# Two graph layers on one core: the opening by half blocks, loads of A at release, chunk ends in three cycles, and a rearranged seam between set-up and first pass

## Chip, core and metric

The kernel runs on one core of a Trainium2 chip. The time is the device time of one execution in microseconds; for a kernel several executions are made and the median is given. The profile is one further execution, recorded by the hardware profiler. Engines are named as in the profile: PE (TensorE, matrix products), DVE (VectorE), ACT (ScalarE), POOL (GpSimd), SP (SyncE). PEld is PE's weight load. SP, ACT and POOL also issue DMA transfers; each issues its own in order.

## The reference, cut to what matters

N is 4096 nodes, F 512 features, H 8 heads of 64. The first layer is graph attention over a dense 0/1 matrix A (`adj`), the second attends within 32 graphs of 128 nodes; both have a residual and a layer norm.

```python
# layer 0
feats   = einsum('nf,hfo->hno', X, W)
s_self  = einsum('hno,ho->hn', feats, a_self)
s_neigh = einsum('hno,ho->hn', feats, a_neigh)
dense = s_self[:, :, None] + s_neigh[:, None, :]
dense = where(dense > 0, dense, 0.2 * dense) * A[None]
attn = softmax(dense, axis=-1)
out = relu(concat_heads(einsum('hij,hjo->hio', attn, feats) + b))
x = layernorm(x + out)
# layer 1
a = where(same_graph, (x Wq^T + bq) (x Wk^T + bk)^T / sqrt(512), 0)
scores = (a + A + A) * where(same_graph, 1, -1e6)
x = layernorm(x + (softmax(scores) * same_graph) @ (x Wv^T + bv))
```

## The kernel before

**Set-up.** The rows of x are taken in 8 blocks of four tiles of 128 rows. `load_rows(k)` loads the four tiles of block k into the pool `xtp`, which has four buffers, so that a block's loads wait for the turning of the one before. `turn_rows(k)` (line 641) transposes them on PE (L650), four tiles by four column groups, and ACT copies the result to `xT` (L653) and sums it on the way. `features(k, u)` (line 715) multiplies a tile by W (L722) into one of two buffers of PSUM; DVE adds b (L733). W has two more columns per head, W a_self and W a_neigh, which DVE computes (L634, L635) from W and from broadcast copies of a_self and a_neigh; with them the product yields the scores too. In block 0 the first three tiles don't wait for these columns: `first_scores` (line 741) gives their scores afterwards, by 24 products of 16 columns (L746). `exponentials` makes e_all, pu_j and d_all; `scaled_features` (line 757) makes g (L766) and f in two parts (L775, L776), which POOL stores in DRAM as g_d and f_d (L789), once for two tiles. `parts_of_exponentials` splits values into bf16 parts on DVE (L676 to L690), `rows_of_exponentials` transposes pu_j and stores pu_d (L695, L699, L703), `columns_of_exponentials` turns the rows back (L708). `partial_sums` and `sums_to_columns` (L561, L568) sum the features over all nodes.

**Passes.** Four passes follow (r, `main_pass`, line 1326), each for two heads. A pass goes over 4 chunks (c) of 1024 targets and, in each, over 32 steps (j) of 128 sources; in the first three passes in cycles of 8 steps, so a chunk has four cycles. In a cycle:

- SP loads f_s and g_s (L1367, L1371), one of each for four steps, into two buffers each. At a chunk's beginning it loads p_row and u_row (L1331, L1334), broadcast rows of pu_d.
- DVE makes q (128 x 1024, L1386) for every step and head. It needs A^T of the step (`at`), p_row and d_all.
- ACT makes mark from q (L1395); for one q of eight DVE does it (L1391).
- PE multiplies f_s with `at` (accf, L1406), g_s with q (acc, L1426) and e_b with mark (dens, L1441); in pass 0 also e_p with `at` (ae, L1350).

**A^T.** In pass 0 `bring` (line 1116) makes `at`. `load_adjacency` (line 577) loads four steps of A for a chunk as fp8 on POOL (L581) into one of three buffers a_b; PE turns two steps at once as bf16 pairs (L1130); ACT casts each to fp32 (L1134); POOL stores it to at_d (L1135), from where SP reads it in later passes. Half of the next cycle's steps are brought behind accf, half at the cycle's end. The tiles `at` and q come from rings of 6 buffers (`ring`, line 550), to which the first three passes add 6 and 2 (`more_at`, `more_q`), in memory that set-up has left.

**Chunk ends.** After a chunk, `sums_to_rows` (line 1171) evacuates accf and acc on DVE (L1180, L1188) and dens and ae on ACT (L1190, L1195). The rest comes in pieces between the next chunk's cycles: transposes and sums of ae (L1203, L1214), those of dens, then the output rows (L1260, L1261) and their store to hs_d (L1271). `run_pieces` gives each cycle a credit, and each piece yields a cost; it runs pieces while the credit is above zero.

**Order.** PE's instructions are issued as the program has them (`manual_schedule`). For the other engines and queues a planner chooses the order when the kernel is built, apart from instructions marked `keep_in_program_order`. The seam in the program is: last features, parts, rows of the last block (L695), L568, columns (L708), then pass 0, which begins by bringing steps 0 to 7. The tile `hst` (pool `hp_`, one buffer) holds both the evacuated ae and the output rows.

Of the kernel before, what the change touches and what calls it, by code (L numbers as in the profile page):

```python
# [19 lines left out]
P = 128  # L20
# [384 lines left out]
def adjacency_streamed_path(  # L405
# [144 lines left out]
    def ring(name, pool, n):  # L550

        if name not in more:
            return pool
        k = turns[name] % (n + more[name][1])
        turns[name] += 1
        return pool if k < n else more[name][0]
# [14 lines left out]

    ats = {}
    a_bs = {}
    pools = {}
# [10 lines left out]

    with tc.tile_pool(name="setup1", bufs=1, side="right") as one, tc.tile_pool(
        name="setup2", bufs=2, side="right"
    ) as two, tc.tile_pool(name="xtp", bufs=4, side="right") as xtp, tc.tile_pool(
        name="setup_rows", bufs=1, side="right"
    ) as late, tc.tile_pool(name="staged", bufs=3, side="right") as staged, tc.tile_pool(  # L590
# [9 lines left out]
        def load_rows(k):  # L600
            xts[k] = []
            for u in range(4):
                xt = xtp.tile([P, F], F32, name="xt_f")
                queue = nc.scalar if k else nc.sync
                queue.dma_start(xt, x[ts(4 * k + u, P), :])
                xts[k].append(xt)

        load_rows(0)
        FW = FH + 2
        w_sb = one.tile([P, FC, H, FW], F32, name="w_sb_f")  # L610
        for c in range(FC):
            nc.scalar.dma_start(
                w_sb[:, c, :, :FH], W[:, ts(c, P), :].rearrange("h p o -> p h o")
            )
        a_b2 = staged.tile([P, PR, 2, 2, FP], F32R, name="fst").bitcast(F32)
        a_b2 = a_b2[:, :2].rearrange("p r u s n -> p (r u s n)").rearrange(
            "p (k h o) -> p k h o", k=2, h=H
        )
        for k, v in enumerate((a_self, a_neigh)):
            nc.sync.dma_start(  # L620
                a_b2[:, k].rearrange("p h o -> p (h o)"), broadcast_rows(v, P, H * FH)
            )
        b_row = one.tile([P, H * FH], F32, name="b_row")
        nc.sync.dma_start(b_row, broadcast_rows(b, P, H * FH))
        b_col = one.tile([P, PR], F32, name="b_col")
# [4 lines left out]
        load_rows(1)  # L630
        for c in range(FC):
            prod = qp.tile([P, C], F32, name="q").rearrange("p (k h o) -> p k h o", k=2, h=H)
            for k in range(2):
                nc.vector.tensor_mul(prod[:, k], w_sb[:, c, :, :FH], a_b2[:, k])  # L634
                nc.vector.tensor_reduce(w_sb[:, c, :, FH + k], prod[:, k], AX.X, OP.add)  # L635
# [3 lines left out]
        xs = one.tile([P, FC, NB], F32, name="xs")  # L639

        def turn_rows(k):
            xT = xTs[k] = two.tile([P, FC, 4, P], F32, name="xT_f")
            pts = {}

            order = [(u, c) for u in range(4) for c in range(FC)]
            for u, c in order if k == 0 else sorted(order, key=lambda x: x[1]):
                if u == 0:
                    last = k == 0 and c == FC - 1
                    pts[c] = misc([P, 4, P]) if last else pss.tile([P, 4, P], F32, name="ps_set")
                nc.tensor.transpose(pts[c][:, u, :], xts[k][u][:, ts(c, P)], ident)  # L650
            for c in range(FC):
                pt = pts[c]
                nc.scalar.activation(  # L653
                    xT[:, c], pt, AF.Identity, accum_out=xs[:, c, k : k + 1]
                )

        def exponentials(k, u, sc):
# [5 lines left out]
            for lo, hi, w in ((0, 3, 1), (3, 5, 0)):  # L663
                nc.vector.tensor_tensor(
# [27 lines left out]
        def rows_of_exponentials(k):  # L692
# [5 lines left out]
            row = rows[k] = late.tile([2 * H, 4 * P], F32, name="pu_row")  # L698
            nc.scalar.copy(  # L699
# [5 lines left out]
        def columns_of_exponentials(k):  # L705
            pc = pss.tile([P, 4, 2 * H], F32, name="ps_set")
# [8 lines left out]
        def features(k, u):  # L715
            pf = psf.tile([P, 2, HB], F32, name="ps_fe")
            pf = pf[:, :, : H * FW // 2].rearrange("p q (h w) -> p q h w", w=FW)
            scored = k > 0 or u == 3
            cols = slice(0, FW if scored else FH)
            for c in range(FC):  # L720
                for q in range(2):
# [6 lines left out]
                    )  # L728
            if u % 2 == 0:
# [11 lines left out]
        def first_scores():  # L741

            ps = pss.tile([P, 4, H, 2], F32, name="ps_set")
            for u in range(3):
# [9 lines left out]
            for u in range(3):  # L754
                exponentials(0, u, ps[:, u].rearrange("p (q h) w -> p q h w", q=2))

        def scaled_features(k, u):
            j, v, i = 4 * k + u, u // 2, u % 2
            fb = sums[k, v][:, i]
            if i == 0:  # L760
                pairs[k, v] = (
                    qp.tile([P, C], F32, name="q").rearrange("p (r u n) -> p r u n", r=PR, u=2),
                    staged.tile([P, PR, 2, 2, FP], F32R, name="fst"),
# [12 lines left out]
            nc.vector.scalar_tensor_tensor(  # L776
# [774 lines left out]
```

## Time and profile before

| | |
|---|---|
| median of 3 runs | 2066.62 us (2066.22 to 2067.95) |
| profiled execution, its time | 2068.04 us |
| its span | 2066.2 us |
| granted PE clock, mean over the span | 0.995 |
| set-up, to the end of the last features | 0 to 156.8 us |
| first accf group starts | 165.2 us |
| first accf group of pass 1 starts | about 592 us |
| ACT busy in 180 to 220 us | 37.45 of 40 us |
| DVE busy in 180 to 220 us | 35.15 of 40 us |
| loads of a_b (L581), issue to landing, median | 16.3 us |
| stores of at_d (L1135), issue to landing, median | 14.9 us |
| DMA read and written | 491.8 and 107.2 MB |

The span runs from the first to the last instruction that the profiler saw. A group row of the profile shows how often a line's instruction ran, its busy time and the mean of one, and the idle time of its engine just ahead of it with what ended that. A row of waits has the total, the number and the longest. A row of windows gives PE, PEld, DVE, ACT and POOL busy time, then the granted PE clock (1.00 is full), the DMA share and GB/s.

### The profile page before, as it was taken

What the parts mean: (1) busy time and instruction counts of PE and PEld (TensorE: products, weight loads), DVE (VectorE), ACT (ScalarE), POOL (GpSimd) and SP (SyncE); (2) the same over time, 40 slices, a digit from 0 to 9 for tenths busy, and PEclk for the clock granted to TensorE, in tenths of its full rate; (3) what the DMA queues carried; (4) which work ended last, traced back from release to release, by engine and by line L of the source; (5) the groups of instructions that cost most, each with busy time, mean ns of one, the idle gap of its engine ahead of it and who ended that gap; (6) DMA issues with size and microseconds to landing.
All of it is one profiled execution on the core that took longest, in us unless ns stands there. A gap on an engine that the chain in (4) does not pass through costs nothing.

```text
span 2066.2 us, 38253 instructions
## 1 busy us (share of the span) xinstructions
PE 2030.9 (98%) x15086; PEld 1049.8 (51%) x15086; DVE 1670.1 (81%) x2125; ACT 1540.4 (75%) x1869; POOL 222.9 (11%) x361
## 2 busy tenths in 40 slices
PE   8999999999999999999999999999999999999997
PEld 6885555444445444444445444444454445445443
DVE  5667888888799998798999899998975884896654
ACT  3338888888878899788899899998885666567420
POOL 1223222222100000000000000000210210210111
PEclk9999999999999999999999999999999999999999
DMA  6989999999899999798999899989974773684211
GB/s 195 303 270 248 270 294 263 296 260 297 264 341 335 367 347 350 258 312 293 327 308 338 300 354 329 329 287 360 315 247 150 240 262 128 229 275 167 74 49 43
DMA packets 207371, 551.31 MB, mean 267 GB/s; under 512 B 24780, under 2 KB 65740, under 8 KB 207180
## 3 DMA queue, kind: packets, MB, share of 16 engines
q1 hardware_dynamic: 136716, 418.45, 58.1%
q0 software_dynamic: 62272, 121.91, 23.1%
q10 hardware_dynamic: 8192, 8.39, 1.2%
q8 instruction: 121, 1.98, 0.4%
q14 instruction: 70, 0.57, 0.1%
HBM read 491.79 MB, written 107.22 MB: 290 GB/s over the span
## 4 chain that ended last, share of the span: by engine, by line
PE 84%; DMA 7%; issue 4%; DVE 2%; ACT 1%; POOL 1%; POOLq 0%; ACTq 0%; DVEq 0%; SPq 0%
PE acc L1426 36%; PE accf L1406 20%; PE ps_m L1067 5%; PE ps_fe L722 5%; PE ps_m L995 5%; DMA at_d<-at 5%; PE dens L1441 5%; PE ps_m L1022 1%; DVE q L1386 1%; PE ps_m L1081 1%; DMA xt_f<-in_x_dram 1%; ACT mark L1395 1%; PE ps_m L975 1%; PE ps_m L1130 1%; PE ps_m L924 1%
## 5 line engine op out<-in xcount | busy, mean ns | idle before, releaser
L1386 DVE SCALAR_TENSOR_TENSOR q<-p_row,d_all,at 128x1024 f32<-128x1024 f32 x1024 | 1241.9, 1277 | 159.9 <-PE acc L1426 129.3
L1395 ACT ACTIVATE mark<-q,nb_all 128x1024 fp8e4<-128x1024 f32 x896 | 995.5, 1145 | 181.4 <-DVE q L1386 165.8
L1426 PE MATMUL acc<-q,g_s 128*32 128x512 f32 x8192 | 904.2, 593 | 1.4 <-DVE q L1386 0.4
L1426 PEld LDWEIGHTS acc<-q,g_s 128*32 128x32 f32 x8192 | 264.3, 110 | 595.3 <-issue 533.6
L1406 PE MATMUL accf<-at,f_s 128*128 128x512 f32 x2048 | 496.7, 398 | 1.9 <-issue 1.8
L1406 PEld LDWEIGHTS accf<-at,f_s 128*128 128x128 f32 x2048 | 380.5, 189 | 111.4 <-issue 28.1
L1151 ACT ACTIVATE ck<-ck,neg_half_f 128x1024 f32<-128x1024 f32 x128 | 146.0, 1141 | 21.7 <-DMA ck<-in_adj_dram 21.7
L1152 ACT ACTIVATE ck<-ck,neg_quarter 128x1024 f32<-128x1024 f32 x128 | 146.4, 1143 | 1.7
L1441 PE MATMUL dens<-mark,e_b 128*6 128x512 fp8e4 x2048 | 125.9, 379 | 0.9 <-ACT mark L1395 0.9
L722 PE MATMUL ps_fe<-w_sb_f,xT_f 128*128 128x264 f32 (+1 forms) x512 | 121.3, 394 | 4.6 <-ACT xT_f L653 4.6
L1134 ACT CAST at<-ps_m 128x1024 fp32r<-128x1024 fp8e4 x128 | 120.1, 1026 | 5.5 <-ACT mark L1395 3.0
L1067 PE MATMUL ps_m<-wvT,x1T 128*128 128x512 f32 x256 | 114.2, 594 | 0.0
L995 PE MATMUL ps_m<-x1T,M_sb 128*128 128x512 f32 x256 | 112.9, 595 | 0.0
L722 PEld LDWEIGHTS ps_fe<-w_sb_f,xT_f 128*128 128x128 f32 x512 | 100.7, 200 | 19.1 <-ACT xT_f L653 5.0
L1271 POOL DMA_DIRECT2D hs_d<-hst x12 | 10.7, 893 | 834.4 <-DVE hst L1261 816.1
L1391 DVE TENSOR_SCALAR mark<-q,d_all 128x1024 fp8e4<-128x1024 f32 x128 | 95.7, 748 | 4.8
L1441 PEld LDWEIGHTS <-e_b 128*6 128x6 bf16 x2048 | 55.8, 86 | 78.5 <-issue 36.2
L1135 POOL DMA_DIRECT2D at_d<-at x128 | 69.0, 539 | 178.0 <-ACT at L1134 107.4
L995 PEld LDWEIGHTS ps_m<-x1T,M_sb 128*128 128x128 f32 x256 | 48.0, 190 | 59.3 <-issue 58.4
L1067 PEld LDWEIGHTS ps_m<-wvT,x1T 128*128 128x128 f32 x256 | 47.6, 190 | 56.4 <-issue 55.1
L1075 DVE TENSOR_TENSOR v_t<-ps_m,bv_row 128x512 f32<-128x512 f32 x32 | 21.7, 683 | 60.5 <-PE ps_m L1067 60.5
L1002 ACT ACTIVATE zT<-ps_m,zb 128x512 f32<-128x512 f32 x32 | 21.8, 680 | 61.1 <-PE ps_m L995 61.1
(185 smaller groups left out, 1084.2 us busy)
## 6 DMA issues: line engine op xcount, KB each, us to landing
at<-at_d SPq DMA_DIRECT2D x384, 512.0 KB, 6.0
f_s<-f_d SPq DMA_DIRECT2D x128, 512.0 KB, 7.5
at_d<-at POOLq DMA_DIRECT2D x128, 512.0 KB, 14.9
ck<-in_adj_dram SPq DMA_DIRECT2D x128, 512.0 KB, 5.4
g_s<-g_d SPq DMA_DIRECT2D x128, 256.0 KB, 5.7
f_d<-fst POOLq DMA_DIRECT2D x16, 1024.0 KB, 7.2
a_b<-in_adj_dram POOLq DMA_DIRECT2D x32, 512.0 KB, 16.3
p_row<-pu_d SPq DMA_DIRECT2D x32, 512.0 KB, 6.7
```

What stands on the lines that cost most here:

```text
L722: nc.tensor.matmul(pf[:, q, :, cols], tile_j(xTs[k][:, c].rearrange("p u n -> p (u n)"), u), w_sb[:, c, 4 * q : 4 * q + 4, cols], start=(c ...
L995: nc.tensor.matmul(pz, L1["M"][:, f, ts(c, P)], x1T[:, f, :], start=(f == 0), stop=(f == FC - 1),)
L1067: nc.tensor.matmul(pv, x1T[:, f, ts(u, P)], L1["wvT"][:, f, :], start=(f == 0), stop=(f == FC - 1),)
L1134: nc.scalar.copy(at, both[:, :, k])
L1151: tc.keep_in_program_order(nc.scalar.activation(ck, ck, AF.Square, bias=neg_half))
L1152: nc.scalar.activation(ck, ck, AF.Abs, bias=neg_quarter, accum_out=binp[:, k : k + 1])
L1386: nc.vector.scalar_tensor_tensor(q, p_row[h], d_j, ats[r, c, j].bitcast(F32), op0=OP.max, op1=OP.mult)
L1391: nc.vector.tensor_scalar(mark, q, d_j, None, op0=OP.is_gt, saturate=False)
L1395: nc.scalar.activation(mark, q, AF.Sigmoid, bias=nb_all[:, j, hh : hh + 1], scale=BIG, saturate=False,)
L1406: nc.tensor.matmul(accf[:, s, :], f_s[j // 4][:, j % 4, w, :], ats[r, c, j][:, ts(s, HB)], start=(j == 0 and w == 0), stop=(j == NT - 1 an ...
L1426: nc.tensor.matmul(acc[o : o + 32, s, :], g_s[j // 4][:, j % 4, h, o % FH : o % FH + 32], qs[j, h][:, ts(s, HB)], start=(j == 0), stop=(j ...
L1441: nc.tensor.matmul(dens[lo : lo + 6, :], e_b[:, j, 2 * r + h, :], marks[j, h][:, ts(s, HB)], start=(j == 0), stop=(j == NT - 1),)
```

## The change

The opening:

- Block 0 is loaded, turned and copied in two halves of two tiles. The second half is turned in the middle of the features of tile 1. Two of W's four loads go to SP; every load of x is on SP; a_self and a_neigh lie in two separate staging buffers. An activation of `neg_quarter` stands ahead of ACT's copies. PE transposes the identity nine times ahead of tile 0 and twice ahead of tile 1.
- All four tiles of block 0 get their scores from `first_scores`, now 32 products, and it runs behind tile 3 (it ran behind tile 2). The score columns of the last two groups of W are pinned on DVE behind the additions of tiles 0 and 1.

The seam:

- Steps 0, 2 and 4 (each with its neighbour) are turned during the last block, behind tiles 1, 2 and 3, and steps 0 to 4 are cast there. Step 6 is turned behind L568, ahead of the last rows. Step 5's cast and the last scaled features are placed behind the copy of these rows; steps 6 and 7 are cast at the beginning of pass 0.
- The first cycle's q and marks are told from which instruction on they may be issued. The last block's `parts_of_exponentials` come behind the q of the first cycle, its columns (L708) behind the first accf.
- Staging is split into pools of one and two buffers, the added `at` buffers into pools of two and four; the order of the set-up pools differs. The first loads of f_s, g_s, p_row and u_row are kept in program order.

The first pass:

- When a block of A has been turned, the load that takes its buffer is issued then, in program order; the loads for steps 12 and 16 of chunk 0 stand at the end of set-up.
- `run_pieces` gets 8 instead of 6 a cycle in pass 0; each piece still yields 6 (the last 1.8).

```diff
+    def turned_steps(c, j, pt):
+        if j % 4 == 0 and (c, j) not in a_bs:
+            load_adjacency(c, j)
...
+        for t in range(CT):
+            nc.tensor.transpose(pt[:, t, :], pairs[:, t, :], ident_b)
+        ahead = c * NT + j + 10
+        if j % 4 == 2 and ahead < NCH * NT and (c or j > 6):
+            tc.keep_in_program_order(load_adjacency(ahead // NT, ahead % NT))
+        return pt
+    def cast_steps(c, j, pt, steps=range(2)):
...
+        for k in steps:
+            at = ats[0, c, j + k] = ring("at", atp, 6).tile([P, C], F32R, name="at")
+            ends_of_setup["ACT"] = nc.scalar.copy(at, both[:, :, k])
+            nc.gpsimd.dma_start(at_d[c, j + k], at.bitcast(F32))
...
-                queue = nc.scalar if k else nc.sync
-                queue.dma_start(xt, x[ts(4 * k + u, P), :])
+                nc.sync.dma_start(xt, x[ts(4 * k + u, P), :])
...
-        load_rows(0)
+        load_rows(0, (0, 1))
...
-            nc.scalar.dma_start(
+            queue = nc.scalar if c < FC // 2 else nc.sync
+            queue.dma_start(
                 w_sb[:, c, :, :FH], W[:, ts(c, P), :].rearrange("h p o -> p h o")
             )
...
+        nc.scalar.activation(neg_quarter, neg_quarter, AF.Identity)
...
+            nc.sync.dma_start(a_s[k], broadcast_rows(v, P, H * FH))
+        load_rows(0, (2, 3))
...
+            def keep_warm(n):
+                pw = psf.tile([P, 2, HB], F32, name="ps_fe")
+                for i in range(n):
+                    nc.tensor.transpose(pw[:, 0, :P], ident, ident)
...
+                if (k, c) == (0, 0) and u < 2:
+                    keep_warm((9, 2)[u])
...
+                if (k, u, c) == (0, 1, 1):
+                    turn_rows(0, (2, 3))
...
-            for u in range(3):
+            for u in range(4):
                 for c in range(FC):
                     nc.tensor.matmul(
                         ps[:, u],
...
+                if k == 0 and u < 2:
+                    score_columns(FC // 2 + u)
-                if u == (0 if k else 2) and k + 1 < NB:
+                if u == (0 if k else 3) and k + 1 < NB:
                     turn_rows(k + 1)
...
+                if k == NB - 1 and u:
+                    bank = ps0 if u == 1 else pss
+                    pt = bank.tile([P, CT, P], BF16, name="ps_m" if u == 1 else "ps_set")
+                    pt = turned_steps(0, 2 * u - 2, pt)
+                    cast_steps(0, 2 * u - 2, pt, range(2 if u < 3 else 1))
...
-        columns_of_exponentials(NB - 1)
+        last_pair = turned_steps(0, 6, misc([P, CT, P], BF16))
+        rows_of_exponentials(NB - 1)
+        with tc.issue_after(ends_of_setup["ROW"].ins):
+            cast_steps(0, 4, pt, range(1, 2))
+            scaled_features(NB - 1, 3)
+        for j in (12, 16):
+            tc.keep_in_program_order(load_adjacency(0, j))
...
-                    run_pieces(0.75 * wide)
+                    run_pieces((0.75 if r else 1.0) * wide)
...
                 if at_step == 0:
-                    for j in cycle:
-                        bring(0, 0, j)
+                    cast_steps(0, 6, last_pair)
...
+                        with following(at_step == 0, ("DVE", 3 if j else 2)):
+                            ends_of_setup["Q"] = nc.vector.scalar_tensor_tensor(
+                                q, p_row[h], d_j, ats[r, c, j].bitcast(F32), op0=OP.max, op1=OP.mult
+                            )
...
+                            with following(at_step == 0, "ACT", "ROW"):
...
+                if at_step == 0:
+                    with following(True, "Q"):
+                        parts_of_exponentials(NT // 4 - 1)
...
+                if at_step == 0:
+                    columns_of_last()
...
+    more["at"], more["q"] = [(atp, 6)], [(qp, 6)]
+    for name, n in (("at", 2), ("at", MORE - 2), ("q", 2)):
+        pool = wide_passes.enter_context(tc.tile_pool(name=f"more_{name}{n}", bufs=n))
+        more[name].append((pool, n))
```

`following` opens `tc.issue_after` for the named instruction, so that what is inside is issued behind it; `in_order` pins an instruction to the program's order.

## The prediction

> **What bounds the kernel now.** I read the page's busy shares first, then TensorE's (PE) own waits, then two-microsecond windows for the granted clock, and last PE's instructions in order of time around the seam between set-up and the first pass.
>
> ```profile
> PE 2030.9 (98%) x15086; PEld 1049.8 (51%) x15086; DVE 1670.1 (81%) x2125; ACT 1540.4 (75%) x1869; POOL 222.9 (11%) x361
> ...
> PE ps_set L650 <- DMA xt_f<-in_x_dram: 6.4, 4, 3.9
> PE ps_fe L722 <- ACT xT_f L653: 4.6, 1, 4.6
> PE ps_m L1130 <- ACT at L1134: 2.0, 2, 1.2
> ...
> PE accf L1406 <- issue: 1.8, 1, 1.8
> PE ps_set L695 <- ACT pu_j L671: 1.3, 1, 1.3
> ```
>
> PE is idle for 2066.2 - 2030.9 = 35.3 us only, and its busy work hardly changes. So the change can win only idle time (each row: total, times, longest, in us) and half-clock time, or create new ones.
>
> ```profile
> 30.00:32.00 2.00, 2.00 (x10) 1.79 (x10) 0.60 (x6) 0.86 (x9) 0.00 (x0) 0.61 0.98 325
> 32.00:34.00 2.00, 2.00 (x6) 1.52 (x6) 0.00 (x0) 0.69 (x3) 0.00 (x0) 0.53 0.41 156
> ...
> 164.00:166.00 2.00, 1.61 (x10) 1.51 (x10) 2.00 (x4) 2.00 (x3) 1.23 (x3) 0.50 1.01 373
> 168.00:170.00 2.00, 2.00 (x6) 1.52 (x5) 2.00 (x2) 2.00 (x3) 0.18 (x1) 0.50 1.02 395
> ```
>
> The third number from the right is the granted clock. In finer windows it is 0.5 from 30.5 to 33.8 (3.4 us) and from 160.1 to 170.4 (10.3 us, three times 3.4): whole stretches of one length. The first follows 24 thin matmuls (L746, 16 columns), during which PE counts as busy; the second follows the patchy seam:
>
> ```profile
> 152.96 3.83 PE L722 MATMUL ps_fe<-w_sb_f,xT_f 128*128 128x264 f32 x16
> 156.63 0.49 PE L695 MATMUL ps_set<-ident_f,pu_j 128*16 128x128 f32 x3
> 158.45 0.28 PE L695 MATMUL ps_set<-ident_f,pu_j 128*16 128x128 f32 x1 [1.33 <-ACT pu_j L671]
> ...
> 159.80 1.59 PE L1130 MATMUL ps_m<-ident_b,a_b 128*128 128x128 bf16 x16
> 162.56 1.01 PE L1130 MATMUL ps_m<-ident_b,a_b 128*128 128x128 bf16 x8 [1.16 <-ACT at L1134]
> 164.39 1.01 PE L1130 MATMUL ps_m<-ident_b,a_b 128*128 128x128 bf16 x8 [0.82 <-ACT at L1134]
> 165.16 9.99 PE L1406 MATMUL accf<-at,f_s 128*128 128x512 f32 x32
> ```
>
> The last features end at 156.8; the first accf group starts 8.4 us later and takes 9.8 us in the chain, against 7.36 us for the next one.
>
> **Start: 4.0 us, from 0 to 8.** In the old order all 16 transposes of x (L650) come first, spread from 3.9 to 9.3 us over four arriving tiles; then PE waits 4.6 us, because ACT, sitting in its queue on loads of the next x tiles, begins its table load at 11.89 and its copies at 13.19. The new order needs two x tiles, has those later loads on SP, and loads the table early. The two x tiles were down by 5.7 us; eight transposes at the cold 0.22 us and a half-width copy (0.6 us for the full width, so about 0.4) put the first features at about 6.7. W is the doubt: its loads took 6.3 to 9.9 us, so I take 7.2. From there: four feature groups at 48 x 0.2156 = 10.35 us per three, so 13.8; the other eight transposes 0.94; the turning of block 1 1.87; scores 32 x 0.1275 (3.06 / 24) = 4.08; the next feature group 3.57. That is 24.3 us warm. To it I add the cold opening, 12.03 - 10.35 = 1.68; about 0.2 of waiting; and 2.2 for a clock drop after the scores (below). End: 7.2 + 28.4 = 35.6, against 39.6 now: 4.0. VectorE (DVE) has 10.9 us of score columns (8 x 1.36) and can start at about 9 us, when a_self is down; with the additions of L733 (0.69 each) between, it ends near 21, before the scores at about 22 to 24. If W or DVE is 4 us late, nothing is won here.
>
> Two rules of the page "TensorE: Matmul & The Clock Gate" speak against this part. **The eleven added warming transposes:** the old trace has PE transposing for 63% of 6.6 to 10.0 us, and the features still run at half speed until about 17 us (matmul records of 797 ns at first, 378 ns later). This leaves open whether full density would have raised the clock. Part 4 of the page, on PE-mode transposes, says that transposes do not engage the full clock. By a reading of the row that blames only the gaps I would save the 1.68 us; by the rule nothing. I take nothing. **The longer scores:** now there are 1.87 us of transposes and 3.06 us of thin matmuls, and one half-clock stretch follows, worth 3.4 x 0.5 = 1.7 us. The new stretch is 5.95 us. Part 1's section on what is happening gives a free-running window of about 3.4 us, which agrees with the stretches above, and which a longer thin stretch fills more surely. One window costs 1.7 us, two cost 3.4; I take 2.2.
>
> **Set-up blocks: 1.2 us, from 0 to 1.3.** Of the 6.4 us that PE waited for x, 1.24 us lie at 92.7: loads issued on ACT at 76.5 to 77.9 landed only at 92.6. They shared the DMA queues with row broadcasts that SP had sent at 73.5 to 76.5 (p_row, u_row). The change pins those, and the first f_s and g_s, behind the x loads on SP, and SP issues x as soon as a buffer is free. What is queued behind a waiting x load is then only needed at the seam, 60 us later.
>
> **Seam: 6.2 us, from 3 to 8.** From the end of the last features (156.79) to the second cycle's accf (193.94) is 37.15 us. Its PE work, warm, is: L695 0.44, L568 0.79, L708 0.35, four turned pairs of steps 1.83, accf 7.36, two pairs 0.91, acc 13.9, dens 1.73, ae 0.92, two pairs 1.0; sum 29.2. Two pairs move into the last set-up block; they cost the same there (0.92 in all). So at most 37.15 - 29.2 = 7.9 us can go: 3.3 us of waits shown above, the rest slow clock. The new order fills the 1.33 us wait for pu_j with a pair of steps, L568 and another pair (0.46 + 0.79 + 0.46). L708 and the parts go behind accf and the Qs. PE then has only about 2.2 us of light work before accf, hardly more than the 1.93 us of a set-up turning that never cost the clock, so no half-clock stretch is expected.
>
> What is late next? *ACT:* five casts (1.02 each) now lie in set-up, where it is busy 6.4 of 20 us. It still owes three casts, a table load (1.28) and 14 marks (1.145 each), 20.4 us with no gap, from about 161.3; so the marks end near 182 to 184, and dens (acc start 168.5 + 13.9) wants them at 182.4. *DVE:* in the old run eight q stood ready 4.5 us before acc; now acc starts 7.5 us sooner, while the first q can start only some 5 us sooner. The sixth q takes the buffer whose g_d store is issued after the last scaled features; stores landed in 4.0 to 7.4 us, so that q comes at about 168 to 169, just before acc, and up to 2 us are lost. I book 1.7 us for both: 7.9 - 1.7 = 6.2. The loads of A for steps 12 and 16 go out on POOL behind these stores; a store of at_d behind them waits 0.9 us each, and its buffer is not needed for a cycle.
>
> **First pass: 2.4 us, from 0.5 to 3.** The old chunk ends spread over four cycles (6 credits a cycle). The last piece falls into the chunk's last cycle: its two DVE products (L1261, 2.56 us) run just ahead of the evacuation of accf (L1180), for which accf at 592.3 waits 1.76 us. Its store of hs_d still holds the buffer that ACT wants for L1195 (12.1 us of waits in all), and dens then waits for marks 0.66 and 0.22 us. With 8 credits the pieces run in cycles one to three, a cycle (26 us) earlier, so both lose their cause: 2.64 us, less something for new small waits. The loads at release win nothing on PE: POOL waited 100.3 us for PE at L581 in the first 560 us, yet PE never waited for a_b. A pinned load follows transposes that its own casts need too, so it delays at_d by its issue alone.
>
> **Sum.** 4.0 + 1.2 + 6.2 + 2.4 = 13.8 us of the profiled span of 2066.2 us, around which 1.8 us lie (its time is 2068.0). That execution was 1.4 us above the median of the runs, 2066.6; I subtract from the median: 2066.6 - 13.8 = **2052.8 us**.
>
> **Rivals.**
> 1. *The cover is thinner* (0.22): DVE or W late at the start (gain 1), q and marks late at the seam (gain 3.5), chunk ends 1.5, blocks 1: 7 us, **2059.6**. For it: ACT is busy 17 to 20 of every 20 us after 160. Against it: eight q buffers, and DVE idle for 6.5 us at 178.
> 2. *The clock stays full* (0.17): dense transposes do raise it (1.7) and the scores do not drop it (2.2), seam near 7.5: 13.8 + 5.2 = 19 us, **2047.6**. For it: set-up turnings of 1.93 us never dropped it. Against: the rule, and the 0.5 at 30.5.
> 3. *Slower: the early A loads choke the seam* (0.05): two blocks of 2 MB in the reference's type, issued back to back at about 161, overtake the last g_d store, and the sixth q waits for a landing like a_b's (16.3 us in the page) in place of 5. The q queue stands, acc comes 11 us late, and PE drops to half clock again (10.3 us, as now, 5 us lost). 16 us against the 13.8: **2069**. It decides the sign once that store lands later than 19 us. Against it: the store goes first on the same queue.
> 4. *The scheduler puts casts or Qs no earlier than before* (0.06): start, blocks and chunk ends alone, about 7.6, less 3 of mixing: **2062**.
>
> The main case has 0.50, its own range 2050 to 2056. For eight in ten I go from 2047.0 to 2060.0, which holds it, most of rivals 1 and 2. Two tenths of a per cent, 4.1 us, is what a measurement here tells from no change. Faster: 0.50 + 0.17 + nearly all of 0.22 and half of rival 4: 0.91; within: 0.05; slower: 0.04.
>
> **What would show it.** Right: the first L722 near 7 us; no wait at L650 near 90; accf's first 32 records in about 7.4 us at clock 1.00, starting some 2.2 us behind the last features; no 1.76 us at the end of the first pass. Wrong: L722 waiting on W or DVE; a half clock behind the last features; q of L1386 waiting on the g_d store; dens waiting on ACT marks in the first cycle by over 2 us.

## The result, and the profile after

| | before | after |
|---|---|---|
| median of 6 runs, us | 2067.21 (2064.97 to 2070.18) | 2055.14 (2053.82 to 2057.91) |
| profiled execution: time, span, us | 2068.04, 2066.2 | 2057.91, 2056.1 |

The changed kernel takes 0.9943 [0.993, 0.9956] of the time, 12.1 us less. The execution that was profiled is the longest of its six, so the two traces differ by 10.1 us only. Both numbers are needed below.

PE's line in the page's busy shares, with the other engines, for the changed kernel:

```profile
PE 2030.4 (99%) x15105; PEld 1051.0 (51%) x15105; DVE 1671.9 (81%) x2125; ACT 1542.2 (75%) x1878; POOL 224.2 (11%) x361
```

PE's work has not changed (2030.9 us before), its idle time went from 35.3 to 25.7 us. PE's own waits of the changed kernel (total, times, longest, in us):

```profile
PE accf L1499 <- ACT at L621: 2.1, 1, 2.1
PE ps_m L1075 <- DVE x1b L520: 1.9, 1, 1.9
PE ps_fe L800 <- ACT xT_f L723: 1.9, 2, 1.6
PE ps_m L610 <- DVE pu_all L787: 1.7, 1, 1.7
PE ps_fe L714 <- POOL ident_f masks.py:199: 1.4, 1, 1.4
PE ps_set L720 <- DMA xt_f<-in_x_dram: 1.0, 3, 0.5
...
```

The waits for x (6.4 us), for the copies of xT (4.6 us) and for the pass boundary ("issue", 1.8 us) have shrunk or gone. Three rows are new. One is the wait of the added warming transposes for the identity (L714), at the very start. The other two lie in the seam: the first accf group (L1499) waits 2.1 us for a cast on ACT, and a turned pair of A (L610) waits 1.7 us for DVE. The granted clock, the third number from the right, in two-microsecond windows of the changed kernel:

```profile
30.00:32.00 2.00, 2.00 (x8) 1.79 (x8) 1.06 (x7) 0.84 (x8) 0.00 (x0) 0.50 0.24 92
32.00:34.00 2.00, 2.00 (x6) 1.49 (x6) 2.00 (x6) 0.62 (x5) 0.18 (x1) 0.50 0.01 4
...
158.00:160.00 2.00, 2.00 (x7) 1.52 (x7) 2.00 (x3) 1.98 (x3) 1.99 (x3) 0.61 0.60 236
160.00:162.00 2.00, 2.00 (x7) 1.58 (x6) 2.00 (x3) 1.99 (x3) 2.00 (x4) 0.54 0.91 317
```

Both half-clock stretches are still there. In one-microsecond windows the one behind the scores lasts from 28.7 to 35.6 (twice 3.4 us, where it was one) and the one of the seam from 158.4 to 161.9 (one, where it was three).

**Where the time went.** I put four marks on PE in both traces and take differences: the turning of block 2 (its first L720), that of block 6, the second cycle's accf, and the first accf of pass 1. Here they are in the kernel before and in the changed one:

```profile
39.47 2.09 PE L650 MATMUL ps_set<-ident_f,xt_f 128*128 128x128 f32 x16
109.53 2.04 PE L650 MATMUL ps_set<-ident_f,xt_f 128*128 128x128 f32 x16
193.75 7.55 PE L1406 MATMUL accf<-at,f_s 128*128 128x512 f32 x32
592.31 7.59 PE L1406 MATMUL accf<-at,f_s 128*128 128x512 f32 x32 [1.76 <-issue]
...
36.76 2.09 PE L720 MATMUL ps_set<-ident_f,xt_f 128*128 128x128 f32 x16
105.36 2.03 PE L720 MATMUL ps_set<-ident_f,xt_f 128*128 128x128 f32 x16
187.43 7.60 PE L1499 MATMUL accf<-at,f_s 128*128 128x512 f32 x32
581.76 7.60 PE L1499 MATMUL accf<-at,f_s 128*128 128x512 f32 x32
```

| stretch of PE | before, us | after, us | gain | forecast |
|---|---|---|---|---|
| start to turning of block 2 | 39.47 | 36.76 | 2.7 | 4.0 |
| to turning of block 6 | 70.06 | 68.60 | 1.46 | 1.2 |
| to second accf (the seam) | 84.22 | 82.07 | 2.15 | 6.2 |
| to first accf of pass 1 | 398.56 | 394.33 | 4.23 | 2.4 |
| rest | 1473.9 | 1474.3 | -0.4 | 0 |

The three middle stretches are firm: in another profile of the changed kernel (e9), and in the experiments that leave them alone, they came out at 68.59 to 68.61, 82.07 to 82.08 and 394.24 to 394.38. The one exception is the seam of e8, with 83.73: there accf ran at full clock, the second of the new waits grew to 3.26 us, and the half clock came behind it. The first stretch is not firm. Over eight profiles with this same opening the mark lies between 33.67 and 37.13, with a mean of 35.1, so against the one profile of the kernel before the gain at the start is 4.3 us on average and 2.7 in the profile shown. The rest, which the change doesn't touch, is not firm either: it lies between 1471.5 and 1474.5 us, with a mean of 1473.0 over the same eight profiles (in the profile shown one more half-clock stretch falls between 1984 and 1988). With the means for both the sum is 4.3 + 1.46 + 2.15 + 4.23 + 0.9 = 13.0. The medians differ by 12.1 here, and by 14.2 when the changed kernel was run again (e9), so the table accounts for the gain to about a microsecond, and not to a tenth.

So the total came out near the forecast by two errors against each other: the seam gave a third of what was booked, and the first pass almost twice. The timeline of the changed kernel at the seam, all engines (start, duration, engine, line, operands; in brackets the idle time before it and what ended it):

```profile
154.64 0.61 PE L610 MATMUL ps_m<-ident_b,a_b 128*128 128x128 bf16 x8
...
155.08 0.60 PE L768 MATMUL ps_set<-ident_f,pu_j 128*16 128x128 f32 x4
...
155.32 1.01 ACT L621 CAST at<-ps_m 128x1024 fp32r<-128x1024 fp8e4 x1
...
156.23 0.59 ACT L777 COPY hst<-ps_set 16x512 f32<-16x512 f32 x1
156.73 0.99 ACT L621 CAST at<-ps_set 128x1024 fp32r<-128x1024 fp8e4 x1
...
157.77 9.18 PE L1499 MATMUL accf<-at,f_s 128*128 128x512 f32 x32 [2.09 <-ACT at L621]
157.90 0.48 DVE L934 MEMSET dens<- 128x512 f32 x1 [1.75 <-ACT at L621]
...
158.89 9.65 DVE L1475 SCALAR_TENSOR_TENSOR q<-p_row,d_all,at 128x1024 f32<-128x1024 f32 x8
...
166.88 0.42 PE L786 MATMUL ps_m<-ident_f,hst 16*128 16x16 f32 x4
...
169.25 0.22 DVE L787 COPY pu_all<-ps_m 128x64 f32<-128x64 f32 x1
169.52 0.61 PE L610 MATMUL ps_m<-ident_b,a_b 128*128 128x128 bf16 x8 [1.67 <-DVE pu_all L787]
```

Read it backwards. The accf group goes over the steps 0 to 7 in order, and the casts of steps 0 to 4 were done by 155, so it had data to begin with. What it has to wait for is ACT reading PSUM, the memory that PE writes its products to: step 5's cast at 156.73 reads a bank of the set-up pool (ps_set), and ACT comes to it only behind the cast of step 6 and the copy of the last rows (the change itself put it behind that copy). The filling of dens with zeros (L934), which reads no data at all, waits for the same cast. (Whether one bank is waited for or the whole set-up pool, the trace doesn't tell.) At the other end of accf, the last columns (L786) go into the shared bank ps_m; DVE copies them out (L787) behind all eight q and a mark of its own, at 169.25, and the next pair of A needs that bank. Neither wait is for data. Between the two lies the half-clock stretch, because of which accf took 9.18 us.

### The profile page after: what moved, and what is told of

It reads as the page before. It is cut to its first block, busy times and chain, and to the rows that moved or that the text cites. A ratio compares the mean times of both kernels' runs of the same rounds, so it can differ in the third digit from the quotient of the medians.

```text
span 2056.1 us, 38302 instructions
## 1 busy us (share of the span) xinstructions
PE 2030.4 (99%) x15105; PEld 1051.0 (51%) x15105; DVE 1671.9 (81%) x2125; ACT 1542.2 (75%) x1878; POOL 224.2 (11%) x361
## 4 chain that ended last, share of the span: by engine, by line
PE 93%; DVE 4%; issue 1%; DMA 1%; SPq 0%; POOL 0%; ACT 0%; POOLq 0%; DVEq 0%
PE acc L1521 41%; PE accf L1499 23%; PE ps_fe L800 5%; PE ps_m L1167 5%; PE dens L1536 5%; PE ps_m L1095 5%; DVE q L1475 3%; PE ps_m L1122 1%; PE ps_m L610 1%; PE ps_m L1181 1%; PE ps_m L1075 1%; PE ps_m L1024 1%; PE ps_m L1339 1%; PE ps_set L720 1%; PE ae L1435 1%
## 5 line engine op out<-in xcount | busy, mean ns | idle before, releaser
L1499 PE MATMUL accf<-at,f_s 128*128 128x512 f32 x2048 | 495.2, 398 | 2.1 <-ACT at L621 2.1
L1499 PEld LDWEIGHTS accf<-at,f_s 128*128 128x128 f32 x2048 | 380.3, 188 | 110.4 <-issue 26.4
L800 PEld LDWEIGHTS ps_fe<-w_sb_f,xT_f 128*128 128x128 f32 x512 | 100.1, 199 | 16.4 <-ACT xT_f L723 2.5
## 6 DMA issues: line engine op xcount, KB each, us to landing
at_d<-at POOLq DMA_DIRECT2D x128, 512.0 KB, 14.8
```

The costliest lines, as they stand in the source:

```text
L800: nc.tensor.matmul(pf[:, q, :, cols], tile_j(xTs[k][:, c].rearrange("p u n -> p (u n)"), u), w_sb[:, c, 4 * q : 4 * q + 4, cols], start=(c ...
L1499: nc.tensor.matmul(accf[:, s, :], f_s[j // 4][:, j % 4, w, :], ats[r, c, j][:, ts(s, HB)], start=(j == 0 and w == 0), stop=(j == NT - 1 an ...
```

## The experiments

A ratio is against the kernel before, run beside it on the same chip: e1 to e4 on one chip, e5 to e8 on a second, e9 to e12 on a third. The changed kernel itself lay 12.1 us under the kernel before in the first runs and 14.2 us in e9's, so a difference of two microseconds between these groups shows nothing.

### Is the wait for step 5's cast, or the columns, what the seam lost?

**Step 5's cast moved up** (e3): both steps of the third pair are cast in set-up.

```diff
-                    cast_steps(0, 2 * u - 2, pt, range(2 if u < 3 else 1))
+                    cast_steps(0, 2 * u - 2, pt)
...
-            cast_steps(0, 4, pt, range(1, 2))
```

> The changed kernel, with step 5's cast right behind step 4's during the last set-up block. Theory A: the wait of accf (2.1 us) and of the dens memset at the seam is for the PSUM bank that step 4 and 5 share, which becomes free only with step 5's cast, held back behind the copy of the last rows; then the wait goes, and with it the half-clock stretch behind it (3.4 us at half speed, 1.7 us): 3 to 4 us faster, 2051 to 2052. Theory B: accf waits because ACT is behind with its casts as a whole; then one cast sooner only shifts the wait to step 6 or 7: within 1 us of 2055.

Measured: 2056.2 us, 0.9951 [0.9937, 0.9964], no gain (e2, beside it, took 2055.4). PE's waits in e3:

```profile
PE ps_m L610 <- DVE pu_all L787: 3.2, 1, 3.2
...
PE accf L1498 <- ACT hst L777: 1.1, 1, 1.1
```

The first wait falls from 2.1 to 1.1 us, and its releaser is now the copy of the last rows into hst, which accf doesn't read at all. So it is the PSUM memory that is waited for, not the cast's result. But accf now ends sooner, the columns reach their bank sooner, and DVE frees it no sooner: the second wait grows from 1.7 to 3.2 us. The half clock moves with it, from 158.4 to 167.2, beside the longer wait.

**The columns moved back** (e4), behind the first turned pairs of the cycle.

```diff
-                if at_step == 0:
-                    columns_of_last()
...
                     bring(*x_)
+                if at_step == 0:
+                    columns_of_last()
```

> The changed kernel, with the last block's columns (four small transposes into the misc bank, evacuated by DVE) put behind the first two pairs of the next cycle instead of ahead of them. Theory A: PE's 1.67 us wait between these pairs is for the misc bank, which DVE evacuates only behind eight q; moved, the wait is gone: 1.7 us faster, about 2053.4. Theory B: DVE's lateness is the limit, and PE then waits for q in acc by as much: no difference, 2055.

Measured: 2057.69 us, 0.9961 [0.9947, 0.9975], no gain. The wait of 1.7 us went, and another came: the columns' own product (L786) waited 2.8 us for a cast on ACT, while accf waited 2.1 us as before. The window of half clock came twice, from 154.3 and from 168.0.

**Both, with the casts of steps 6 and 7 behind the row copy and the columns behind the whole acc group** (e7):

```diff
-                    cast_steps(0, 2 * u - 2, pt, range(2 if u < 3 else 1))
+                    cast_steps(0, 2 * u - 2, pt)
...
-            cast_steps(0, 4, pt, range(1, 2))
...
-                    cast_steps(0, 6, last_pair)
+                    with following(True, "ROW"):
+                        cast_steps(0, 6, last_pair)
...
-                if at_step == 0:
-                    columns_of_last()
...
+                if at_step == 0:
+                    columns_of_last()
                 if r == 0:
                     pieces(c, j0 // 4, 1)
```

> The changed kernel with three edits at the seam together: step 5 is cast right behind step 4, the casts of steps 6 and 7 come behind the copy of the last rows, and the last block's columns come behind the first acc. Theory A (accf waits for PSUM banks that ACT frees late, and the second pair for the misc bank that DVE frees late; each mended alone showed the other in its place): both waits and the half clock behind them go, and acc starts 3.5 to 5 us earlier; 3 us or more faster than the changed kernel, about 2051.5. Theory B (DVE and ACT bound the first cycle: 16 q of 1.28 us and 14 marks of 1.15 us): what is won ahead of acc is lost in acc and dens; within 1 us of 2055.

Measured: 2052.34 us, 0.9933 [0.9919, 0.9946]. PE's timeline in e7 at the same place:

```profile
154.53 7.62 PE L1499 MATMUL accf<-at,f_s 128*128 128x512 f32 x32 [1.06 <-ACT hst L777]
162.00 1.07 PE L610 MATMUL ps_m<-ident_b,a_b 128*128 128x128 bf16 x16
162.99 14.63 PE L1519 MATMUL acc<-q,g_s 128*32 128x512 f32 x128
177.55 0.42 PE L786 MATMUL ps_m<-ident_f,hst 16*128 16x16 f32 x4
```

One wait of 1.06 us is left, accf takes 7.62 us at full clock, and the stretch from the turning of block 6 to the second accf is 78.38 us in place of 82.07: 3.7 us. The two waits give 1.0 and 1.7 of it, accf at full clock 1.6, and an acc group of 14.63 in place of 13.94 us takes 0.7 back. The medians alone would not show this: 2052.34 is 3.0 us less than e5 on the same chip, but the ratio is the same as e9's. The firm evidence is the stretch in the trace, and e12 below, which has the same seam and ran beside e9. It takes the mends together: step 5's cast alone and the columns alone handed their gain to the next bank. The third edit was not tried by itself.

### Chunk ends, and loads at release

**Chunk ends over four cycles again** (e1), all else as changed:

```diff
-                    run_pieces((0.75 if r else 1.0) * wide)
+                    run_pieces(0.75 * wide)
```

> The changed kernel, but with 6 credits a cycle in pass 0 as before, so that a chunk's pieces run over four cycles again; all else is the changed kernel. Theory A (from the two traces: pass 0 is 4.2 us shorter in the changed kernel, and the idle of PE that went, 0.66 + 0.22 + 1.76 us, is only part of it): 4 us above the changed kernel, about 2059. Theory B (the prediction: only the idle counts): 2.4 us above, about 2057.5. Rival (the loads at release shorten pass 0, not the chunk ends): no difference, 2055. In its trace A and B want the wait at accf in front of pass 1 and dens waiting for marks to come back.

Measured: 2069.95 us, 1.0014 [1.0008, 1.0021]. This is longer than the kernel before, and 14.8 us above the changed kernel, a size that neither expectation had. The timeline of e1 in the first cycle of the third chunk:

```profile
386.79 0.59 ACT L1274 COPY hst<-ae 128x512 f32<-128x512 f32 x1 [9.52 <-DMA hs_d<-hst]
387.27 3.23 ACT L1485 ACTIVATE mark<-q,nb_all 128x1024 fp8e4<-128x1024 f32 x3
...
397.31 0.38 PE L1536 MATMUL dens<-mark,e_b 128*6 128x512 fp8e4 x1 [0.65 <-ACT mark L1485]
```

ACT stood 9.5 us until a store of hs_d let go of the buffer it copies into. All its marks came that much later, and dens could only follow one mark at a time. The clock answers to the patches, as these windows of e1 show in the next chunk:

```profile
510.00:512.00 2.00, 0.74 (x8) 0.17 (x4) 2.00 (x4) 2.00 (x3) 0.00 (x0) 1.00 1.03 376
...
514.00:516.00 2.00, 1.56 (x15) 0.44 (x17) 2.00 (x3) 2.00 (x3) 0.00 (x0) 0.50 1.23 128
...
518.00:520.00 2.00, 2.00 (x14) 1.81 (x12) 1.79 (x2) 2.00 (x4) 0.00 (x0) 0.50 1.03 346
```

PE is busy for a third of its time, and then at half clock for almost seven microseconds. The first two stores of hs_d landed in 16.4 and 14.6 us in e1; in the kernel before, with the chunk ends in four cycles too, in 11.3 and 10.5. (The third, at the end of the pass, took 8.1 and 6.1.) What differs in this part between the two is when A is loaded, which the next two kernels try.

**Loads of A at need** (e5), and **both undone** (e6):

```diff
-        ahead = c * NT + j + 10
-        if j % 4 == 2 and ahead < NCH * NT and (c or j > 6):
-            tc.keep_in_program_order(load_adjacency(ahead // NT, ahead % NT))
...
-        for j in (12, 16):
-            tc.keep_in_program_order(load_adjacency(0, j))
```

> The changed kernel, but each block of A is loaded when its first step is brought, as before, and the two loads at the end of set-up are gone; chunk ends stay in three cycles. Theory A (from the run with four cycles, where the hs_d store took 15.5 us to land against 10.5 before and ACT waited 9.5 us for it: the loads at release crowd the chunk's end, and only the three cycles take the store out of their way): loads at release win nothing by themselves; about 2055, within 1.5 us of the changed kernel. Theory B (the loads at release shorten pass 0): 2 to 4 us slower, 2057 to 2059.

> The changed kernel with both edits of pass 0 undone: loads at need and chunk ends over four cycles. Theory A (the 14 us that the four cycles cost came from the loads at release beside them): pass 0 is as in the kernel before, 2.4 to 4.2 us above the changed kernel, 2057.5 to 2059.5, and the dens waits are a few tenths of a us, not 6 us. Theory B (the new seam makes ACT late in every chunk, so that four cycles cost 14 us whatever the loads do): about 2069 again.

Measured: e5 2055.33 us, 0.9949 [0.9935, 0.9963]; e6 2060.96 us, 0.9971 [0.996, 0.9981]. So the four versions of the first pass are, in us:

| | chunk ends in three cycles | in four |
|---|---|---|
| loads at release | 2055.1 | 2070.0 (e1) |
| loads at need | 2055.3 (e5) | 2061.0 (e6) |

Loads at release win nothing: the first pass takes 394.27 us in e5 and 394.33 in the changed kernel. With chunk ends in four cycles they cost 9 us (e1 against e6). The wait that grows is ACT's for the store of hs_d, 9.5 us in the worst case against 5.2 us in e6, where the first two stores landed in 11.8 and 10.2 us. That the time of the loads causes this is shown, as the two programs differ in nothing else; how they slow the store is not. In e1 a block of A sent 15 us ahead of the first store was still landing for 9 of the store's 16 us, in e6 one for 3 of 12; but in e6 another block went out 1.6 us behind the store. With three cycles that store is sent a cycle earlier (its landing took 6.2 to 8.0 us) and ACT never waited for it. The chunk ends by themselves are worth 5.6 us by e6 against e5. The two profiles differ by 6.0, of which 1.3 us lie in the start, which the edit doesn't touch; on the stretch of the first pass alone it is 398.89 - 394.27 = 4.6 us.

### The opening

**No warming transposes** (e2):

```diff
-                if (k, c) == (0, 0) and u < 2:
-                    keep_warm((9, 2)[u])
```

> The changed kernel without the eleven warming transposes of the identity. Theory A (the trace: the second x tile's transposes take 272 ns a record as warm ones do, so transposes do raise the clock): the first features run at half clock again until a full busy stretch of 3.4 us has passed, records of about 797 ns at first, about 1.7 us longer to the end of the first features; most of it reaches the end: 2056 to 2057. Theory B (the rule, taken in the prediction: transposes don't raise the clock): no difference, 2055.

Measured: 2055.43 us, 0.9943 [0.993, 0.9957]: no difference.

**The changed kernel once more** (e9), as the measure for the kernels beside it.

> The changed kernel itself, as the measure for the other three of this call: 2055, within 1 us of its first median, if the chip matters little.

Measured: 2053.52 us, 0.9933 [0.9919, 0.9946], 14.2 us less than the kernel before beside it. With it I can compare two executions of one program. PE's timeline of the changed kernel's profile shown above, in the opening:

```profile
5.69 0.55 PE L720 MATMUL ps_set<-ident_f,xt_f 128*128 128x128 f32 x3 [0.51 <-DMA xt_f<-in_x_dram]
...
6.58 5.52 PE L800 MATMUL ps_fe<-w_sb_f,xT_f 128*128 128x256 f32 x24 [0.24 <-ACT xT_f L723]
...
17.07 7.18 PE L800 MATMUL ps_fe<-w_sb_f,xT_f 128*128 128x256 f32 x32 [1.62 <-ACT xT_f L723]
...
26.05 4.86 PE L826 MATMUL ps_set<-w_sb_f,xT_f 128*128 128x16 f32 x32
30.74 6.18 PE L800 MATMUL ps_fe<-w_sb_f,xT_f 128*128 128x264 f32 x16
```

And the same view of e9:

```profile
5.63 0.90 PE L720 MATMUL ps_set<-ident_f,xt_f 128*128 128x128 f32 x3 [0.31 <-DMA xt_f<-in_x_dram]
...
6.67 7.68 PE L800 MATMUL ps_fe<-w_sb_f,xT_f 128*128 128x256 f32 x24
...
17.26 7.18 PE L800 MATMUL ps_fe<-w_sb_f,xT_f 128*128 128x256 f32 x32 [0.30 <-ACT xT_f L723]
...
26.23 3.94 PE L826 MATMUL ps_set<-w_sb_f,xT_f 128*128 128x16 f32 x32
30.03 3.81 PE L800 MATMUL ps_fe<-w_sb_f,xT_f 128*128 128x264 f32 x16
```

In the first, the transposes had become fast by 5.7 us (0.55 us for three, against 0.90), and the first 24 feature products took 5.52 us; in the second they ran slow and took 7.68. (The column of the granted clock reads 1.00 all through the opening in both; that the slow ones ran at half clock is read from the durations.) It won nothing: the warm run then waited 1.62 us for ACT's copies, and both came to the last 32 feature products and to the scores within 0.2 us of each other. The roles are reversed at the thin scores (16 columns each): here e9 kept the full clock, and the other lost 3.3 us up to the turning of block 2. Of the eight profiles with this opening, four had no half clock behind the scores, two had one window and two had two. The mark at the turning of block 2 follows them: 33.67 to 34.55 us with none, 34.95 and 35.80 with one, 36.76 and 37.13 with two. One program's time varies by this much from the start alone.

**Block 0 loaded and turned whole** (e10); **x on ACT's queue from block 1 on** (e11):

```diff
-        load_rows(0, (0, 1))
+        load_rows(0)
...
-        load_rows(0, (2, 3))
...
-                if (k, u, c) == (0, 1, 1):
-                    turn_rows(0, (2, 3))
...
-        turn_rows(0, (0, 1))
+        turn_rows(0)
```

```diff
-                nc.sync.dma_start(xt, x[ts(4 * k + u, P), :])
+                queue = nc.scalar if k else nc.sync
+                queue.dma_start(xt, x[ts(4 * k + u, P), :])
```

> The changed kernel, but with block 0 loaded, turned and copied as a whole ahead of the first features; W on two queues, the early table load, the loads on SP, the warming and the order of the scores stay. Theory A (the half blocks are what starts the features sooner): the first features begin at about 9.5 us in place of 6.6, less the 0.94 us of transposes that lie ahead of them: 2 us slower, 2057. Theory B (what held the old opening up was ACT's queue, not the number of tiles; x and W arrive when they arrive): within 1 us of the changed kernel.

> The changed kernel, with the loads of x from block 1 on issued by ACT's queue as before. Theory A (ACT stands still in its queue until an x buffer is free, late for the copies of the opening): the first features begin later and wait for copies, 2 to 4 us slower, 2057 to 2059. Theory B (with the early table load and the pinned p_row loads the queue no longer matters): 2055.

Measured: e10 2057.15 us, 0.9945 [0.9932, 0.9959], 3.6 us above e9; e11 2059.03 us, 0.9956 [0.9942, 0.9969], 5.5 us above it. In e10 the features begin at 9.72 instead of 6.67. In e11 the timeline shows what a load does in the queue of an engine that also computes:

```profile
8.16 1.49 ACTq L653 DMA_DIRECT2D xt_f<-in_x_dram  x2
9.69 0.38 ACT L724 ACTIVATE xT_f<-ps_set 128x256 f32<-128x256 f32 x1 [6.35 <-DMA w_sb_f<-in_L_gnn_W_dram]
...
10.22 4.10 PE L801 MATMUL ps_fe<-w_sb_f,xT_f 128*128 128x256 f32 x9 [3.31 <-ACT xT_f L724]
```

ACT stands until its two loads are issued at 8.16 to 9.65, the copies come behind them, and PE waits 3.31 us. Both of the start's causes are thus real. The two costs together are more than the 4.3 us of the start. Both profiles also had two windows of half clock behind the scores; how much of the cost is theirs was not settled.

**Scores in two halves** (e8): 16 thin products behind the turning of block 1, 16 behind the next feature group, so that neither stretch is long.

```diff
-        def first_scores():
+        def first_scores(us):
...
-            for u in range(4):
+            for u in us:
...
+                if u == 0 and k == 1:
+                    first_scores((2, 3))
+                    for v in (2, 3):
+                        scaled_features(0, v)
+                    parts_of_exponentials(0)
...
-                    first_scores()
-                    for v in range(3):
+                    first_scores((0, 1))
+                    for v in range(2):
```

> The changed kernel, with the 32 thin score products split: 16 behind the turning of block 1, 16 behind the first features of block 1, so that no light stretch is longer than 3.9 us. Theory A (a window of about 3.4 us filled by thin products and transposes halves the clock; the long stretch of 6 us fills one for sure): the half clock behind the scores goes or is one window instead of two, 1.7 to 3.4 us faster, 2052 to 2053.5. Theory B (the clock drops anyway, since 3.9 us still fills a window, and later scores delay DVE): no difference, 2055.

Measured: 2052.99 us, 0.9936 [0.9922, 0.9949]. Its profile has no half clock there, but that alone shows little, as half of the unsplit ones have none either. Its time can't be told from e9's 2053.52, so what the split is worth stays open.

### Put together

e12 has e7's seam, e8's scores, and ACT's copies of block 0 pinned in program order, so that the activation of fst can't stand ahead of them.

```diff
+                in_order(k == 0, ins)
...
-            nc.scalar.activation(fst[:, :, i, 0, :], fr, AF.Copy, scale=-1.0)
+            in_order(k == 0, nc.scalar.activation(fst[:, :, i, 0, :], fr, AF.Copy, scale=-1.0))
```

> The changed kernel with the mended seam, the split scores, and ACT's copies of block 0 and its f copies kept in program order, so that no f copy stands ahead of a copy that PE waits for. Theory A (the gains are in different places and add): 3 from the seam, 2 from the scores, 0.5 to 1.5 from the copies: 2049 to 2050. Theory B (the first cycle is bound by DVE and ACT, which a sooner start only pushes against): no better than the mended seam, 2052.

Measured: 2049.89 us (2048.85 to 2050.85), 0.9912 [0.9897, 0.9927]: 17.8 us less than the kernel before and 3.6 less than e9, the shortest of all. Its stretch of the seam is 78.35 us, 3.7 less than e9's, which is the whole difference. At the turning of block 6 it was 0.2 us behind e9, so its profile shows no gain from the split scores and the pinned copies.

## Why the prediction was right, and where it was not

**Start, 4.0 us: right on average, by the causes given.** The features began at 6.58 (7.2 was taken, for W's sake), and nothing waited for W or the score columns. The first turned tiles, SP's queue and the early table load did what was worked out (e10, e11). Unforeseen was an activation of fst that was issued on ACT ahead of the second half's copies, with a wait of 8.4 us for its addition; it cost PE the 1.62 us of the row above. The clock drop behind the scores was booked at 2.2 us; over eight profiles it was none to two windows, with a mean of 0.75 windows, 1.3 us.

**The rule on transposes: the value was right, its reason only in part.** In 3 of 12 profiles with the added transposes these alone brought the full clock before any feature product had run (three transposes of x in 0.55 or 0.56 us in place of 0.90), against Part 4 of "TensorE: Matmul & The Clock Gate" of the Trainium skill. The 1.68 us that I considered and refused was then really gained (7.68 - 5.52 = 2.2 us by the rows above) and given back within ten microseconds at the copies. So the warming can work, but it won nothing: in nine of twelve profiles it brought no full clock, in two of the three others the copies took the gain back (waits of 1.62 and, in e5, 1.75 us), and e2 without it is no slower.

**Set-up blocks, 1.2 us: right.** 1.46 us; no wait for x is left behind the opening.

**Seam, 6.2 us: this is the step that failed.** From 7.9 us of idle and half-clock time I kept back 1.7 us, with the sentence "PE then has only about 2.2 us of light work before accf [...] so no half-clock stretch is expected". The light work was as said, from 153.32 to 155.68. But 2.09 us of standing came behind it, then half a clock for one window (1.7 us), then 1.67 us more: 5.5 us in place of 1.7, which leaves the 2.15 us measured and little over. Of the signs named, the half clock behind the last features, a sign of being wrong, came; accf in 7.4 us at full clock, a sign of being right, did not. I had asked what is late next on ACT and DVE by following data: marks, q, the store of g_d. All three were in time: the eight q ran one behind the other, and no dens waited in the first cycle. What was late was memory in PSUM: two banks, one held by a cast that ACT ran third in line, one by a copy that stood behind eight q on DVE. e7 and e12 show it: with the banks freed in time the stretch is 3.7 us shorter, of the 4.0 that were missing.

**First pass, 2.4 us: the mechanism right, the size too small.** It was 4.23 us in the trace and 4.6 by undoing it. The 1.76 us at the pass boundary went as booked. The dens waits were mis-sized: their rows said 0.66 and 0.22 us, but the cycles that hold them took 27.03 and 26.19 us against 25.8 for a cycle without, so 1.6 us. A dens group that follows its marks one at a time also runs longer in records that count as busy: in the kernel before 28 products took 2.07 us, where 32 usually take 1.91. And the two accf groups next to these took 7.98 and 7.96 us in place of 7.6, another 0.8; both are back in e6, at 8.00 and 7.97. That makes 1.76 + 1.6 + 0.8 = 4.2. The first of the two places in the kernel before:

```profile
399.57 2.07 PE L1441 MATMUL dens<-mark,e_b 128*6 128x512 fp8e4 x28
402.30 0.39 PE L1441 MATMUL dens<-mark,e_b 128*6 128x512 fp8e4 x4 [0.66 <-ACT mark L1395]
...
404.41 7.98 PE L1406 MATMUL accf<-at,f_s 128*128 128x512 f32 x32
```

Why these accf groups run longer is not shown.

**Loads at release, nothing: right alone, incomplete together.** That they make the shorter chunk ends necessary (e1 against e6, 9 us) was not seen. It is the rival of the early loads at another place than I put it: at the seam the stores of g_d were in time, in the first pass the stores of hs_d are not, once they are sent a cycle later.

**The sum.** 13.8 us were forecast and 12.1 came. The seam lacked 4.0 of them and the first pass gave 1.8 more than booked, the start (by its mean) and the blocks 0.6. That these cancel to within two microseconds is luck. The median lies 2.3 us above the forecast, 0.6 of it because the kernel before ran that much longer in these runs.

## What to carry to other kernels

When work is pulled together, follow each tile's memory as well as its data: for every accumulator and staging bank, ask which engine reads it last and what stands ahead of that read in its queue. Where one such wait stands behind another, mend them together: here either mend alone won nothing, since the next bank in line took what it gave. And two changes that share a queue or a buffer should be undone singly and both: here one won nothing and the other 5 us, and the first without the second cost 9.

## What was not expected of the hardware

- The clock can drop though PE counts as busy all the time: 16 transposes (2.0 us) and 32 products of 16 columns (3.94 us at full clock) follow one another, and half clock came on or behind them, for 3.4 or 6.8 us, in 4 of 8 profiles of one opening. Which of the two kinds of work brings it, no run here separates.
- In the opening and at the seam of all the profiles, half clock comes in whole stretches of about 3.4 us (3.4, 6.8 or 10.2). Which piece of PE's patchy work pays for it varies: with the same waits ahead of accf, e9 had it from 154.6, as accf began, and e8 not there but from 167.8, behind a wait of 3.26 us for the columns.
- With chunk ends in four cycles a store of 512 KB landed in 11.8 and 10.2 us (e6) or in 16.4 and 14.6 us (e1), and only the times at which blocks of A are loaded differ between the two.
